# Cross-attention over 32 batches on one core: the issue order of five engines for batches 2 to 30 taken from one table

## The chip, the cores and the metric

The kernel runs on one core of one Trainium2 chip. The core has TensorE (PE; its weight loads are listed as PEld), VectorE (DVE), ScalarE (ACT), GpSimd (POOL) and SyncE (SP); here nearly all transfers are started from SP's queue. The metric is device time in microseconds, and less is better. Each engine works through its own instructions in the order in which the program lists them, and waits at an instruction until what it needs from the others is there.

## The reference

`x` has 32 batches of 512 rows by 640 columns, the context 32 by 77 rows by 1024 columns. All 77 context rows are text, so of the reference's four attentions three run over no rows at all, and their contribution is nothing. What is left:

```python
residual = hidden_states
q = _heads(hidden_states @ to_q_w)            # 20 heads of 32
h_txt = _sdpa(q, _heads(ehs_txt @ to_k_w), _heads(ehs_txt @ to_v_w))
...
out = _merge(h_txt) + SCALE_OBJ * _merge(h_obj) + SCALE_OTH * _merge(h_oth) + SCALE_IP * _merge(h_ip)
out = out @ to_out_w + to_out_b
out = (out + residual) / RESCALE
```

with `_sdpa` the softmax of q.k / sqrt(32) over the 77 keys, times v.

## The kernel before, in words

**Numbers.** Each operand of a product is kept as a high part in the reduced format `fp32r` and a low part, the rest; a product is three matmuls, high by high, high by low and low by high (`PAIRS`). An operation "high" copies (a cast), an operation "low" subtracts.

**Stages.** First the context's keys and values are made for all batches and put to DRAM (`k_dram`, `v_dram`). Then the 32 batches run, each in five chunks of 128 columns, four heads each: chunk n = 5 b + j, one call of `slot(n)` each (L688 to L825). At last `end()` drains what still runs behind.

**One chunk.** A chunk's work lies over several slots, so a slot holds work of several chunks:

- *Queries* of the next chunk, `queries(n + 1)` (L437): five steps of three matmuls of 512 columns into `pq`. `split_q` (L451) then makes `qt`: a cast of the whole on ACT (L454), two half copies on POOL (L458), two half subtractions on DVE (L460).
- *Scores* of this chunk, `scores(n, t)` (L464) for four row tiles t: three short matmuls into a bank `sc` (three banks), then the maximum on DVE (L486). `exps` (L491): four exponentials on ACT into `pn`, each with its sum.
- *Probabilities* of chunk n - 1: reciprocals on DVE (`sums`, L506), `normalize` on POOL (L511), `transpose_p` (L515): a transposition in blocks on DVE into the one buffer `z` (L518), four stores to DRAM (`pd`, L525).
- *Rows* of chunk n - 3 come back with `load_p` (L531, two transfers into `raw`). Of chunk n - 4: `cast_p` on ACT (L542, L543), `last_p` on POOL (L556), `rest_p` on DVE (L549) make `pp`.
- *Values* of chunk n - 4 (L564): six passes of 512 columns into `pa`. `sum_a` (L578): a copy `aw` of the lower half on ACT (L581) and two additions on DVE (L583). One slot later `high_a` (L585) on ACT and `low_a` (L593, L595) on DVE make `at`, which also empties `pa` (one buffer).
- *Output* of an earlier batch: 40 steps of three matmuls of 320 columns (`project`, L611) into two banks `po`, eight steps a slot in two pieces; batch b - 1 in chunks 3 and 4, batch b - 2 in chunks 0 to 2. A closed bank is added to the residual on DVE (L642) and stored.
- *x of the next batch*: loaded in four quarters into the one buffer `xs` (L253), turned in four parts on DVE (`transpose_x`, L257), split on ACT (L264) and POOL (L265).
- *Keys and values* of a group of chunks are reloaded in many small transfers (L419, L432); POOL copies two blocks of the keys (L423, L424).

**What sets the order.** `tc.manual_schedule` makes the order of the calls the order on each engine. In `slot` PE has: a score triple, two query steps, a triple, three query steps, a triple, then a piece of output, the values, a triple and a second piece of output. In chunks 1 and 4 the first piece stands one place earlier. Each of these groups is issued in one go. On DVE, `rest_p` stands before `low_a`, except in chunk 4. `load_p` stands in the middle of the slot, and the casts of its rows at the start of the next.

Of the kernel before, what the change touches and what calls it, by code (L numbers as in the profile page):

```python
# [51 lines left out]
def kernel(  # L52
# [358 lines left out]
    def load_keys(b, g, heads=range(HPC)):  # L411
        j0, nj = GROUPS[g]
        src = k_dram[g][:, :, :, b * NKEY : (b + 1) * NKEY].bitcast(F32)
        kb = kbs[g].bitcast(F32)
        for i in heads:
            own, half = slice(i * HD, (i + 1) * HD), slice(i % 2 * NKEY, (i % 2 + 1) * NKEY)
            other = slice(*((i + 2) % HPC * HD + k for k in (0, HD)))
            for part, rows in enumerate((own, other)):
                nc.sync.dma_start(kb[rows, 1 + i // 2, :, half], src[own, part])  # L419

    def copy_keys(g):
        kb = kbs[g]
        nc.gpsimd.tensor_copy(kb[:64, 0], kb[:64, 1].bitcast(F32))  # L423
        nc.gpsimd.tensor_copy(kb[64:, 3], kb[64:, 2].bitcast(F32))  # L424
# [39 lines left out]
    def scores(n, t):  # L464
# [6 lines left out]
        for m, (cols, keys_) in enumerate(  # L471
            (
                (slice(0, KCOLS), kb[:, 0::3, jg]),
                (slice(0, half), kb[:, 1, jg]),
                (slice(half, KCOLS), kb[:, 2, jg]),
            )
        ):
            nc.tensor.matmul(  # L478
                sc[:, cols],
                qt[:, m, t * P : (t + 1) * P],  # L480
                keys_,
                start=(m == 0),
                stop=(m == 2),
            )
# [30 lines left out]
    def transpose_p(n):  # L515

# [5 lines left out]
        pd = dram.tile([(NBLK + 2) * Q, S], F32, tag="pd", name="pd", bufs=6)  # L522
        rows = pd[: NBLK * Q].rearrange("(b i) q -> i b q", i=Q)
        for a in range(4):
            nc.sync.dma_start(  # L525
                rows[:, :, a * P : (a + 1) * P],
                z[a * Q : (a + 1) * Q].rearrange("p b t j -> p b (t j)"),
            )
        pds[n] = pd

    def load_p(n):  # L531
        pd = pds.pop(n)
        raw = late[0].tile([P, 3, S], F32, tag="raw", name="raw", bufs=2)
        nc.sync.dma_start(raw[:, 0:2, :], pd.rearrange("(k p) q -> p k q", k=2)[:P])
        nc.sync.dma_start(raw[:64, 2, :], pd[P : P + 64, :])
        raws[n] = raw

    def cast_p(n):

        raw = raws[n]  # L540
        pp = late[0].tile([P, 5, S], FPR, tag="pp", name="pp", bufs=1)
        nc.scalar.copy(pp[:64, 4, :], raw[:64, 2, :])  # L542
        nc.scalar.copy(pp[:, 0:2, :], raw[:, 0:2, :])  # L543
# [20 lines left out]
    def values(n):  # L564
        b, j = divmod(n, NC_)
        g = GROUP_OF[j]
        pp, vb = pps.pop(n), vbs[g][:, j - GROUPS[g][0]]
        pas[n] = late[1].tile([P, 2, S], F32, tag="pa", name="pa", bufs=1)
        for p, t, c in PASSES:
            nc.tensor.matmul(  # L570
                pas[n][:, p, :],
                vb[:, p, t, :],
                pp[:, c, :],
                start=(c == p),
                stop=(c == p + 2),
            )

    def sum_a(n):  # L578
        pa = pas[n]
        aw = late[0].tile([64, 2, S], F32, tag="aw", name="aw", bufs=1)  # L580
        nc.scalar.copy(aw, pa[64:])  # L581
        for p in range(2):
            nc.vector.tensor_tensor(pa[64 * p : 64 * p + 64, 0], pa[:64, p], aw[:, p], ALU.add)  # L583
# [9 lines left out]
    def low_a(n):  # L593
        at = ats[n]
        nc.vector.tensor_tensor(  # L595
            at[:, 1, :], pas.pop(n)[:, 0], at[:, 0, :].bitcast(F32), ALU.subtract
# [38 lines left out]

    def finish():

        while closed:
# [3 lines left out]
            nc.vector.tensor_tensor(  # L642
                xr[:, cols], pos.pop((b, t, h))[:, :HALF], xr[:, cols], ALU.add
            )
# [181 lines left out]

    def end():
# [105 lines left out]
    for n in range(LATE, N):  # L933
# [42 lines left out]
```

## Time and profile before

| what | value |
|---|---|
| runs | 1919.91, 1916.11, 1912.5 us |
| median | 1916.11 us |
| span of the profiled execution | 1928.2 us (its own time outside the span is not recorded) |
| mean granted TensorE clock | 0.995 |
| HBM traffic over the span | 222 GB/s |

Span and busy times are of one execution under the profiler, from its first to its last instruction. A row of groups reads: line, engine, operation, output<-inputs, shapes, count, then busy us and mean ns of one, then the idle time of the engine before them and what ended it. The chain of waits that ended last gives these shares of the span:

```profile
PE 38%; DMA 22%; ACT 14%; DVE 9%; SPq 7%; POOL 5%; issue 5%; ACTq 0%; DVEq 0%; POOLq 0%
```

No single engine or line holds it: it changes hands between all of them.

### The profile page before, as it was taken

What the parts mean: (1) busy time and instruction counts of PE and PEld (TensorE: products, weight loads), DVE (VectorE), ACT (ScalarE), POOL (GpSimd) and SP (SyncE); (2) the same over time, 40 slices, a digit from 0 to 9 for tenths busy, and PEclk for the clock granted to TensorE, in tenths of its full rate; (3) what the DMA queues carried; (4) which work ended last, traced back from release to release, by engine and by line L of the source; (5) the groups of instructions that cost most, each with busy time, mean ns of one, the idle gap of its engine ahead of it and who ended that gap; (6) DMA issues with size and microseconds to landing.
All of it is one profiled execution on the core that took longest, in us unless ns stands there. A gap on an engine that the chain in (4) does not pass through costs nothing.

```text
span 1928.2 us, 37543 instructions
## 1 busy us (share of the span) xinstructions
PE 1882.9 (98%) x10332; PEld 1663.1 (86%) x10332; DVE 1619.6 (84%) x2494; ACT 1527.4 (79%) x6210; POOL 1423.9 (74%) x1116
## 2 busy tenths in 40 slices
PE   9999997999999999999999999999999999999997
PEld 7888896898888888888888888988888888888887
DVE  4444447899999999999999999999999899999885
ACT  3232248998889898898898889998999889989883
POOL 1100067888888888888888888888888888888874
PEclk9999998999999999999999999999999999999999
DMA  9978868989999899888998998988889989988875
GB/s 185 205 194 248 198 180 218 229 232 234 233 225 235 231 232 225 229 234 231 233 231 228 228 238 236 237 231 232 237 232 227 228 223 232 227 231 229 225 202 166
DMA packets 565022, 431.36 MB, mean 224 GB/s; under 512 B 191120, under 2 KB 473168, under 8 KB 564816
## 3 DMA queue, kind: packets, MB, share of 16 engines
q1 hardware_dynamic: 559760, 413.62, 84.9%
q0 software_dynamic: 4416, 14.34, 2.2%
q8 instruction: 85, 1.39, 0.3%
q14 instruction: 121, 0.99, 0.2%
q10 hardware_dynamic: 640, 1.02, 0.2%
HBM read 247.17 MB, written 181.64 MB: 222 GB/s over the span
## 4 chain that ended last, share of the span: by engine, by line
PE 38%; DMA 22%; ACT 14%; DVE 9%; SPq 7%; POOL 5%; issue 5%; ACTq 0%; DVEq 0%; POOLq 0%
PE po L613 10%; PE pq L443 9%; DMA raw<-pd 8%; DMA xs<-in_x_dram 7%; ACT pn L496 6%; PE pv L191 5%; PE pk L191 5%; PE pa L570 4%; PE sc L478 4%; DVE pp L549 3%; DMA kb<-k_dram 2%; ACT pp L543 2%; SPq L432 2%; ACT pp L542 1%; ACT xt L264 1%
## 5 line engine op out<-in xcount | busy, mean ns | idle before, releaser
L496 ACT ACTIVATE pn<-sc,nm 128x77 f32<-128x77 f32 x2560 | 793.8, 332 | 46.6 <-DVE nm L486 40.6
L613 PE MATMUL po<-wo_s,at 128*128 128x320 f32 x3840 | 635.1, 314 | 12.1 <-DVE at L595 9.0
L443 PE MATMUL pq<-xt,wq_s 128*128 128x512 f32 x2400 | 623.7, 401 | 0.0
L613 PEld LDWEIGHTS po<-wo_s,at 128*128 128x128 f32 x3840 | 568.3, 189 | 20.4 <-DVE at L595 17.4
L496 ACT ACTIVATION_READ_ACCUMULATOR pn<-sc,nm 128x1 f32 x2560 | 544.6, 213 | 0.0
L511 POOL TENSOR_TENSOR pn<-pn,rs 128x1232 f32<-128x1232 f32 x160 | 507.7, 3173 | 33.3 <-DVE rs L506 24.2
L443 PEld LDWEIGHTS pq<-xt,wq_s 128*128 128x128 f32 x2400 | 431.3, 190 | 76.1
L478 PEld LDWEIGHTS sc<-kb,qt 128*128 128x128 f32 x1920 | 327.8, 189 | 57.2 <-POOL qt L458 8.7
L478 PE MATMUL sc<-kb,qt 128*128 128x154 f32 (+1 forms) x1920 | 318.1, 274 | 11.0 <-POOL qt L458 4.5
L486 DVE TENSOR_REDUCE nm<-sc 128x4 f32<-128x308 f32 x640 | 287.7, 450 | 37.7 <-PE sc L478 33.2
L549 DVE TENSOR_TENSOR pp<-raw,pp 128x1024 fp32r<-128x1024 f32 x160 | 253.1, 1582 | 40.7 <-ACT pp L543 38.7
L556 POOL TENSOR_TENSOR pp<-raw,pp 64x512 fp32r<-64x512 f32 x160 | 209.3, 1308 | 100.2 <-ACT pp L542 90.5
L570 PE MATMUL pa<-pp,vb 128*128 128x512 f32 x960 | 263.7, 404 | 15.3 <-DVE at L595 10.1
L518 DVE STREAM_TRANSPOSE z<-pn 128x1280 f32<-128x1280 f32 x160 | 241.8, 1511 | 9.3 <-DMA pd<-z 2.7
L460 DVE TENSOR_TENSOR qt<-pq,qt 64x512 fp32r<-64x512 f32 x320 | 219.1, 685 | 29.0 <-ACT qt L454 22.7
L583 DVE TENSOR_TENSOR pa<-pa,aw 64x512 f32<-64x512 f32 x320 | 222.6, 696 | 24.3 <-ACT aw L581 14.0
L265 POOL TENSOR_TENSOR xt<-xs,xt 128x512 fp32r<-128x512 f32 x160 | 202.6, 1291 | 37.1 <-ACT xt L264 32.5
L570 PEld LDWEIGHTS pa<-pp,vb 128*128 128x128 f32 x960 | 169.7, 188 | 63.4 <-DVE pp L549 15.4
L606 POOL TENSOR_TENSOR xr<-xr,bias 128x640 f32<-128x640 f32 x128 | 202.7, 1585 | 17.3 <-DMA xr<-in_x_dram 5.4
L458 POOL CAST qt<-qt 64x512 fp32r<-64x512 f32 x320 | 194.8, 609 | 23.7 <-ACT qt L454 4.2
L581 ACT COPY aw<-pa 64x1024 f32<-64x1024 f32 x160 | 161.9, 1012 | 48.2 <-PE pa L570 44.1
L542 ACT CAST pp<-raw 64x512 fp32r<-64x512 f32 x160 | 99.5, 622 | 99.7 <-DMA raw<-pd 95.6
(46 smaller groups left out, 1640.9 us busy)
## 6 DMA issues: line engine op xcount, KB each, us to landing
pd<-z SPq DMA_DIRECT2D x640, 160.0 KB, 3.5
raw<-pd SPq DMA_DIRECT2D x160, 512.0 KB, 4.3
xs<-in_x_dram SPq DMA_DIRECT2D x128, 320.0 KB, 7.4
xr<-in_x_dram SPq DMA_DIRECT2D x128, 320.0 KB, 3.7
out_dram<-xr SPq DMA_DIRECT2D x127, 320.0 KB, 3.7
raw<-pd SPq DMA_DIRECT2D x160, 128.0 KB, 4.3
v_dram<-vs SPq DMA_DIRECT2D x80, 192.0 KB, 4.0
k_dram<-ks POOLq DMA_DIRECT2D x20, 512.0 KB, 4.2
```

What stands on the lines that cost most here:

```text
L443: nc.tensor.matmul(pqs[n], wq_s[:, k, a, j * P : (j + 1) * P], xts[b, k][:, c, :], start=(k == 0 and m == 0), stop=(k == NC_ - 1 and m == 2),)
L460: nc.vector.tensor_tensor(qt[r, 1 + w, :], pq[r], qt[r, 0, :].bitcast(F32), ALU.subtract)
L478: nc.tensor.matmul(sc[:, cols], qt[:, m, t * P : (t + 1) * P], keys_, start=(m == 0), stop=(m == 2),)
L486: nc.vector.tensor_reduce(nm, sc[:, :KCOLS].rearrange("p (h k) -> p h k", k=NKEY), AX.X, ALU.max, negate=True)
L496: nc.scalar.activation(pnb[n % 2][:, at, :NKEY], sc[:, i * NKEY : (i + 1) * NKEY], AF.Exp, bias=nm[:, i : i + 1], accum_out=sms[n][:, at : ...
L511: nc.gpsimd.tensor_tensor(pf, pf, rs.unsqueeze(2).to_broadcast([P, NQ * HPC, NKEY]), ALU.mult)
L518: nc.vector.transpose(z.rearrange("p b t j -> p t b j"), pn.rearrange("p (t h) k -> p t (h k)", t=NQ).rearrange("p t (b i) -> p t b i", i=Q),)
L549: nc.vector.tensor_tensor(pp[:, 2:4, :], raw[:, 0:2, :], pp[:, 0:2, :].bitcast(F32), ALU.subtract)
L556: nc.gpsimd.tensor_tensor(pp[64:, 4, :], raw[:64, 2, :], pp[:64, 4, :].bitcast(F32), ALU.subtract)
L570: nc.tensor.matmul(pas[n][:, p, :], vb[:, p, t, :], pp[:, c, :], start=(c == p), stop=(c == p + 2),)
L583: nc.vector.tensor_tensor(pa[64 * p : 64 * p + 64, 0], pa[:64, p], aw[:, p], ALU.add)
L613: nc.tensor.matmul(pos[b, t, h][:, :HALF], ats[b * NC_ + j][:, a, t * P : (t + 1) * P], wos[0][:, j, c, h * HALF : (h + 1) * HALF], start= ...
```

## The change

`slot` stays for chunks 0 to 9 and for the last batch. For batches 2 to 30 a table `PLAN` of 344 steps is walked once a batch, and `issue` carries out each. A step is the chunk j (0 to 4), a letter, and arguments. To make single steps possible, several helpers are cut in two or more (`split_x` into `high_x` and `low_x`, `scores` into `score_tile` and `score_max`, `load_keys` by head and part, `transpose_p` into `block_transpose` and `store_p`, `values` into `value_pass`, `sum_a` into `lower_half` and `add_halves`, `finish` into `add_output` and `store_output`); what each does is the same as before.

Letters: `q` a query step of the next chunk, `s` a score triple, `v` a value pass, `p` an output step by its number in `STEPS`; `m` maximum, `e` exponentials, `r` reciprocals, `N` normalize, `z` block transposition, `w` a store of it; `d` load of rows (0: 512 KB, 1: 128 KB), `c` cast of rows, `l` `last_p`, `R` `rest_p`; `A` and `a` `sum_a` in its parts, `h` and `L` high and low of `at` of chunk n - 5; `Q`, `k`, `g` the parts of `split_q`; `f` and `o` addition and store of the output, `b` bias; `T`, `X`, `x` turn and split of x; `K` copy of keys; `ur`, `ux`, `uk`, `uv` loads of residual, x, keys and values.

```diff
+    PLAN = (
+        "0p16 0s0 0q0 0s1 0m0 0q1 0h 1uv13 0r 0m1 0c1 0N 0q2 0L 0d0 1uv16 0p17 0e0 0f10 0d1 0q3 0R "
+        "0uk101 0s2 0c0 0uk100 0q4 0m2 0ux3 0v1 0l 0Q 0uk130 0v0 0p18 0e1 0g1 0p19 0p20 0k0 0g0 0s3 "
+        "0e2 0v2 0f11 0k1 0v4 0m3 0v3 0o1 0p21 0b2 0z 0uk110 0v5 1q0 0uk111 0A 1s0 1s1 0w1 0e3 0a1 "
+        "1q1 0w3 0T0 0p22 0w2 1q2 1c0 1d0 1r 0a0 1c1 0w0 1q3 1l 1m0 1uv12 1T1 0p23 1h 1uv17 1q4 1e0 "
+        "1m1 1N 1uv15 1L 1p24 0ur3 1s2 1R 1d1 1Q 1p25 1uv14 1e1 1s3 1v0 1m2 1v1 1v3 1m3 1p26 1e2 "
+        "1uv10 1g0 1k1 1v5 1p27 0uk120 1f20 1k0 1v2 1uv11 1g1 1e3 1p28 2d0 1v4 1z 0uk131 1p30 1b3 2s0 "
+        "1A 2s1 2q0 2r 1w2 2c0 1a0 2q1 1ur0 2c1 2l 0uk121 1a1 2s2 2d1 1p31 2m0 2h 1w1 2q2 2m1 2e0 2N "
+        "1w0 2m2 2q3 2L 2uv06 2q4 2R 2e1 1p29 2v0 2f21 2s3 2Q 2v1 1T2 3uk030 2e2 2p32 2k0 1w3 2v2 2g0 "
+        "2p35 2o2 2k1 2v3 2T3 2v4 1K11 3uk021 2v5 2p33 2g1 3uk020 1K10 2A 2p36 2b0 2uv03 2m3 2p37 "
+        "2uv07 2X0 2p38 2a0 3uk011 2X1 3q0 3d0 2z 2x0 3c1 3d1 3s0 3q1 2e3 2x1 2p34 2w0 2a1 3s1 2w2 "
+        "3m0 2p39 3c0 3uk031 2f30 3q2 3m1 3h 2uv01 3l 3r 3q3 3e0 3L 2w1 3uk000 3q4 3N 2w3 3X2 3s2 "
+        "2uv00 3p0 3X3 3m2 3s3 3f31 3Q 3v0 3R 3v1 3o3 3e1 3v3 3uk001 3p4 2uv02 3p1 3g0 4d0 3p5 3e2 "
+        "3k1 2uv05 3p6 3g1 3k0 3v2 2uv04 3p2 3z 3X4 4K01 4d1 3v5 3p7 3x2 3v4 4s0 3m3 3A 3w3 3p3 3x3 "
+        "3w0 4q0 3w1 3e3 3a1 4q1 3w2 3x4 3a0 4s1 3ur1 4q2 4m0 3uk010 4h 4r 4m1 4ur2 4c0 4s2 4L 4q3 "
+        "4ux0 4c1 4l 4ux1 4p8 4e0 4ux2 4p9 4f00 4q4 4N 4m2 4f01 4p10 4Q 4R 4o0 4v1 4e1 4v0 4v2 4p11 "
+        "4g0 4v3 4p12 4e2 4g1 4p13 4k0 4s3 4z 4v5 4K00 4v4 4p14 4A 4k1 4p15 4m3 4w2 4b1 4a0 4e3 4w0 "
+        "4w3 4a1 4w1 "
+    ).split()
+    ADDED = {4: 1, 0: 2, 1: 2, 2: 2, 3: 2}
+    OPEN = [(B - 3, 1, 0)]
+
+    scs, nms, rss = {}, {}, {}
+
+    def issue(b, token):
+
+        j, op, arg = int(token[0]), token[1], [int(c) for c in token[2:] if c.isdigit()]
+        n, kind = b * NC_ + j, token[2:3]
+        old, out_b = n - LAG, b - PIECES[j][0]
+        half = (slice(0, 64), slice(64, P))
+        if op == "q":
+            queries(n + 1, arg[0], arg[0] + 1)
+        elif op == "s":
+            scs[n, arg[0]] = score_tile(n, arg[0])
+        elif op == "m":
+            nms[n, arg[0]] = score_max(scs[n, arg[0]])
+        elif op == "e":
+            exps(n, arg[0], scs.pop((n, arg[0])), nms.pop((n, arg[0])))
+        elif op == "r":
+            rss[n - 1] = sums(n - 1)
+        elif op == "N":
+            normalize(n - 1, rss.pop(n - 1))
+        elif op == "z":
+            block_transpose(n - 1)
+        elif op == "w":
+            store_p(n - 1, arg[0])
+        elif op == "d":
+            load_rows(n - LAG + 1, arg[0])
+        elif op == "c":
+            cast_rows(old, arg[0])
+        elif op == "l":
+            last_p(old)
+        elif op == "R":
+            rest_p(old)
+        elif op == "v":
+            value_pass(old, arg[0])
+        elif op == "A":
+            lower_half(old)
+        elif op == "a":
+            add_halves(old, arg[0])
+        elif op == "h":
+            high_a(old - 1)
+        elif op == "L":
+            low_a(old - 1)
+        elif op == "Q":
+            nc.scalar.copy(qts[(n + 1) % 2][:, 0, :], pqs[n + 1])
+        elif op == "k":
+            qt, w = qts[(n + 1) % 2], arg[0]
+            nc.gpsimd.tensor_copy(qt[half[1 - w], 1 + w, :], qt[half[w], 0, :].bitcast(F32))
+        elif op == "g":
+            qt, w = qts[(n + 1) % 2], arg[0]
+            nc.vector.tensor_tensor(
+                qt[half[w], 1 + w, :], pqs[n + 1][half[w]], qt[half[w], 0, :].bitcast(F32), ALU.subtract
+            )
+        elif op == "p":
+            t, h, c = STEPS[arg[0] if len(arg) == 1 else 10 * arg[0] + arg[1]]
+            if c == 0:
+                output_bank(out_b, t, h)
+            project(out_b, t, h, c)
+        elif op == "f":
+            add_output(b - ADDED[j], *arg)
+        elif op == "o":
+            store_output(b - ADDED[j], arg[0])
+        elif op == "b":
+            add_bias(b - BIAS[j][0], arg[0])
+        elif op == "T":
+            transpose_x(b + 1, arg[0])
+        elif op == "X":
+            high_x(b + 1, arg[0])
+        elif op == "x":
+            low_x(b + 1, arg[0])
+        elif op == "K":
+            copy_half_keys(*arg)
+        elif kind == "r":
+            load_residual(b - RESIDUAL[j][0], arg[0])
+        elif kind == "x":
+            ahead = 1 if arg[0] == 3 else 2
+            if b + ahead < B:
+                load_x(b + ahead, arg)
+        elif kind == "k":
+            load_head_keys(b + 1 if j == 3 else b, *arg)
+        elif kind == "v":
+            load_values(b - 1 if j == 1 else b, arg[0], SEGMENTS[arg[1] : arg[1] + 1])
+
```

The loop:

```diff
-    for n in range(LATE, N):
+    for n in range(LATE, 2 * NC_):
+        slot(n)
+    for b in range(2, B - 1):
+        while closed:
+            closed.pop()
+        for token in PLAN:
+            issue(b, token)
+    closed.extend(OPEN)
+    for n in range(N - NC_, N):
         slot(n)
     end()
```

On PE the query steps, output steps, value passes and triples now stand singly or in short runs between each other. The second piece of output is not kept in order of its steps everywhere: chunk 3 has 0, 4, 1, 5, 6, 2, 7, 3, and chunk 2 has 32, 35, 33, 36, 37, 38, 34, 39. Value passes and additions change places with their neighbours in some chunks. `rest_p` stands behind `low_a` in all chunks. On SP the four stores of `z`, the loads of rows, and the loads of keys and values are spread between each other, one transfer a step.

More of the change, by code (lines that the diff above doesn't have):

```diff
@@ L562, with value_pass, values, lower_half @@
     PASSES = [(p, t, c + p * (t == 0)) for t, c in ((0, 0), (1, 4), (0, 2)) for p in range(2)]
[L564 removed]
+    def value_pass(n, i):
         b, j = divmod(n, NC_)
         g = GROUP_OF[j]
[L567 to L576, printed above, removed]
[L578 to L583 removed]
+        pp, vb = pps[n], vbs[g][:, j - GROUPS[g][0]]
+        if n not in pas:
+            pas[n] = late[1].tile([P, 2, S], F32, tag="pa", name="pa", bufs=1)
+        p, t, c = PASSES[i]
+        nc.tensor.matmul(
+            pas[n][:, p, :],
+            vb[:, p, t, :],
+            pp[:, c, :],
+            start=(c == p),
+            stop=(c == p + 2),
+        )
+    def values(n):
+        for i in range(len(PASSES)):
+            value_pass(n, i)
+    def lower_half(n):
+        aws[n] = late[0].tile([64, 2, S], F32, tag="aw", name="aw", bufs=1)
+        nc.scalar.copy(aws[n], pas[n][64:])
+    def add_halves(n, p):
+        pa, aw = pas[n], aws[n]
+        nc.vector.tensor_tensor(pa[64 * p : 64 * p + 64, 0], pa[:64, p], aw[:, p], ALU.add)
+    def sum_a(n):
+        lower_half(n)
+        add_halves(n, 0)
+        add_halves(n, 1)
     def high_a(n):
```

119 lines of the change are left out of this document (77 added, 42 removed).

## The prediction

> **What bounds the kernel now.** I read the page's first part, then the windows by stage, then TensorE (PE) in order of time, then the waits of the steady stretch, 400 to 1800 us, which is clear of the opening (keys and values for all batches) and of the tail.
>
> ```profile
> PE 1882.9 (98%) x10332; PEld 1663.1 (86%) x10332; DVE 1619.6 (84%) x2494; ACT 1527.4 (79%) x6210; POOL 1423.9 (74%) x1116
> ```
>
> PE is the engine to look at. Two windows over the steady stretch, the first for products into `po` alone (PE, PEld and DVE busy), the second for everything (PE, PEld, DVE, ACT, POOL busy; granted clock, DMA share, GB/s):
>
> ```profile
> 400.00:1800.00 1400.00, 549.90 (x3321) 489.94 (x3321) 101.47 (x222) 1.00 0.90 231
> ...
> 400.00:1800.00 1400.00, 1382.88 (x7884) 1233.37 (x7884) 1294.04 (x1993) 1253.68 (x5258) 1196.39 (x913) 1.00 0.90 231
> ```
>
> A batch has 40 steps of 3 output products, so 3321/120 = 27.7 batches lie in 1400 us: **50.6 us a batch**. Per batch DVE is busy 46.7, ACT 45.3, POOL 43.2 us, the DMA engines 0.90 of the time; the clock was 1.00, so no clock gain is to be had. Nothing beside PE binds by its sum, but DVE has under 4 us to spare.
>
> How much of the 50.6 is products? A busy PE overstates it, because matmul ends are modelled, so I go by starts (columns: start us, us, engine, line, shapes, count):
>
> ```profile
> 1006.44 1.56 PE L570 MATMUL pa<-pp,vb 128*128 128x512 f32 x6
> 1007.84 0.48 PE L478 MATMUL sc<-kb,qt 128*128 128x308 f32 x3
> 1008.15 1.96 PE L613 MATMUL po<-wo_s,at 128*128 128x320 f32 x12
> 1009.95 0.49 PE L478 MATMUL sc<-kb,qt 128*128 128x308 f32 x3
> 1010.28 1.59 PE L443 MATMUL pq<-xt,wq_s 128*128 128x512 f32 x6
> 1011.71 0.50 PE L478 MATMUL sc<-kb,qt 128*128 128x308 f32 x3
> 1012.04 2.26 PE L443 MATMUL pq<-xt,wq_s 128*128 128x512 f32 x9
> 1014.14 0.49 PE L478 MATMUL sc<-kb,qt 128*128 128x308 f32 x3
> ```
>
> From start to next start: 6 value passes 1.40, 12 output products 1.80, 6 query products 1.43, 9 of them 2.10, a score triple about 0.325. A chunk is 15 query, 24 output, 6 value products and 4 triples: 1.43 + 2.10 + 2 x 1.80 + 1.40 + 4 x 0.325 = 9.83 us; five are 49.2 us. So **PE stands still about 1.4 us a batch**. Where, is told by one stop in order of time and by the waits of the steady stretch (waited for: us, times, longest):
>
> ```profile
> 1055.45 1.81 PE L613 MATMUL po<-wo_s,at 128*128 128x320 f32 x11
> 1057.62 0.41 PE L613 MATMUL po<-wo_s,at 128*128 128x320 f32 x1 [0.36 <-DVE at L595]
> ```
>
> ```profile
> ACT pp L542 <- DMA raw<-pd: 88.9, 78, 3.0
> POOL kb L424 <- DMA kb<-k_dram: 72.3, 28, 4.1
> ...
> PEld po L613 <- DVE at L595: 14.4, 24, 1.4
> PEld pa L570 <- DVE pp L549: 14.0, 28, 0.6
> ...
> PEld pa L570 <- DVE at L595: 10.4, 21, 1.8
> ...
> PEld pa L570 <- POOL pp L556: 2.1, 4, 0.8
> ```
>
> Three places: output products of chunk 3 that need the low part of `at` just made (`low_a`, L595); value passes of chunks 1 and 2 that need `pa` emptied by the same line; value passes of chunk 4 that come before `rest_p` (L549) is through. ACT and POOL wait too, for rows and keys from DRAM, and so run late into these.
>
> **The change, part by part.** No arithmetic is added, no transfer, no product: all counts stay. What moves is the order on each engine and on SP's queue, for batches 2 to 30 (29 of 32). So the most that PE can gain is 29 x 1.4 = 41 us, and each edit is priced by what PE has between a producer and its user.
>
> *Output steps and `low_a`, chunk 3.* Step 3 (chunk 3's input) was fourth; in the table `3L` is followed by one query step, two triples, seven other output steps, six passes and another triple before `3p3`: 0.7 + 0.65 + 7 x 0.45 + 1.4 + 0.33 = 6.2 us of PE. `3L` costs 0.68. This stop goes.
>
> *Passes behind `low_a`.* Between `1L` and `1v0`: two output steps, two triples, 1.55 us; between `2L` and `2v0`: two query steps and an output step, 1.85 us. The rest of DVE that stands ahead of `L` counts too, below.
>
> *Passes behind `rest_p`, chunk 4.* The passes are split: `4v1 4v0 4v2 4v3` and three output steps and a triple stand between `4R` and `4v5`: 0.93 + 1.35 + 0.33 = 2.6 us against 1.6 for L549. Goes.
>
> *Rows and keys.* Counting the PE steps between them in the table, loads `d` stand five to thirteen us ahead of their casts `c`, against 4.4 to 9.8 us for the slowest kind of load, x (rows below); the 88.9 and 72.3 us of waits on ACT and POOL (3.2 and 2.6 us a batch) turn into spare time. That cover is what lets the steps above be early; alone it moves PE by nothing.
>
> *The new waits.* `2s0`, the first triple of chunk 2, reads what `1g1` writes, and everything PE has left is queued behind it. I add up DVE from there back. Its groups in the steady stretch, with mean ns, then how closely two follow:
>
> ```profile
> L486 DVE TENSOR_REDUCE nm<-sc 128x4 f32<-128x308 f32 x554 | 248.8, 449 | 28.0 <-PE sc L478 24.0
> ...
> L549 DVE TENSOR_TENSOR pp<-raw,pp 128x1024 fp32r<-128x1024 f32 x138 | 220.1, 1595 | 36.1 <-ACT pp L543 34.3 <-DMA pd<-z 1.6
> L518 DVE STREAM_TRANSPOSE z<-pn 128x1280 f32<-128x1280 f32 x138 | 208.6, 1511 | 6.5 <-DMA pd<-z 1.2 <-POOL xr L606 0.9
> L583 DVE TENSOR_TENSOR pa<-pa,aw 64x512 f32<-64x512 f32 x276 | 192.0, 696 | 9.0
> L460 DVE TENSOR_TENSOR qt<-pq,qt 64x512 fp32r<-64x512 f32 x278 | 190.3, 684 | 20.2 <-ACT qt L454 14.7
> ...
> L581 ACT COPY aw<-pa 64x1024 f32<-64x1024 f32 x139 | 140.6, 1012 | 24.7 <-PE pa L570 21.0 <-PE sc L478 1.1
> L642 DVE TENSOR_TENSOR xr<-po,xr 128x320 f32<-128x320 f32 x222 | 101.5, 467 | 0.0
> L595 DVE TENSOR_TENSOR at<-pa,at 128x512 fp32r<-128x512 f32 x139 | 94.5, 680 | 5.8 <-ACT at L590 5.8
> L257 DVE STREAM_TRANSPOSE xs<-xs 128x640 f32<-128x640 f32 x110 | 91.0, 827 | 0.0
> ```
>
> ```profile
> L506 DVE RECIPROCAL rs<-sm 128x16 f32<-128x16 f32 x160 | 37.0, 231 | 0.4
> ```
>
> ```profile
> 1031.15 1.43 DVE L583 TENSOR_TENSOR pa<-pa,aw 64x512 f32<-64x512 f32 x2
> 1032.49 0.83 DVE L257 STREAM_TRANSPOSE xs<-xs 128x640 f32<-128x640 f32 x1
> ```
>
> Two of L583 take 1.34 from start to start, so one follows 0.03 to 0.08 us before the last has ended. From `0T0` to `1g1` stand 2 x 0.83, 0.23 (reciprocal, the last row), 0.70, 4 x 0.45, 0.68, 1.60, 2 x 0.68 and 0.47, which is 8.5, with overlap 7.6 to 8.2. Before them the copy `0A` (1.0, after `0v5`) and `0a1` (0.7). From the end of `0v5` to `2s0` PE has one full chunk, 9.83. That is 9.3 to 9.9 plus a few tenths of handing over: the slack is about **0.2 us**, and this holds only if `0T0` does not wait.
>
> It may. `0T0` turns part of the next batch's x, whose fourth quarter `0ux3` is issued on SP behind four stores of `z` and six more transfers, all after `4z`:
>
> ```profile
> 1010.64 2.90 SPq L525 DMA_DIRECT2D pd<-z  x4
> 1013.65 0.43 SPq L534 DMA_DIRECT2D raw<-pd  x1
> 1014.12 0.58 SPq L535 DMA_DIRECT2D raw<-pd  x1
> ...
> 1021.03 2.27 SPq L525 DMA_DIRECT2D pd<-z  x4
> ```
>
> ```profile
> DMA to landing us min/median/max: 4.4/7.5/9.8
> ...
> DMA to landing us min/median/max: 5.9/5.9/5.9
> ...
> DMA to landing us min/median/max: 5.0/5.0/5.0
> ```
>
> (The first landing line is of all x loads of the steady stretch, the other two of a fourth quarter alone, issued at 1024 and at 1075 us.) Four stores take 2.3 to 2.9 us to issue, six more about 0.5 each: 5.6. With the 5.0 to 5.9 of a fourth quarter x is there 10.6 to 11.5 us after `4z`. DVE between `4z` and `0T0`: five L486, three L583, two L642, L595, L549, two L460, one L518 and a reciprocal, 10.6 us, with overlap 9.6 to 10.3, and about 0.4 of waiting for `0Q` and `0A`: 10.0 to 10.7. So `0T0` waits 0 to 1.5 us, I take 0.7; less the slack of 0.2 that is a stop of 0.5 a batch. With a landing at 7.5, the median of all x loads, the wait is 2.7.
>
> [...]
>
> *Other tight spots.* Between `4L` (0.68) and `4p8`, which reads it, PE has one query step, 0.7; between POOL's `4k1` and `0s0` two output steps, 0.9, but `4k1` is last behind `4l`, `4N`, `4k0` and `4K00`. From below they cost nothing, if those covers hold; from above, what such waits cost before on the PEld rows: 14.4 and 10.4 us over 27.7 batches, 0.5 and 0.4 a batch. I take 0.25 for both, nearer to nothing, since each still has a step as cover.
>
> **Sum.** 1.4 - 0.5 - 0.25 = 0.65 us a batch; x 29 = 19 us. The profiled execution spans 1928.2 us; the median of the runs is 1916.11, or 0.9937 of it. (1928.2 - 19) x 0.9937 = 1897 us.
>
> **Rivals.** *All stops gone* (x lands by 10 us, DVE keeps its overlap): 1.4 x 29 = 41, 1928.2 - 41 = 1887, x 0.9937 = 1875 us. For it: the least landing, 4.4; against it: DVE without a gap over half a batch.
>
> *One set of stops for another:* `0T0` waits about 1.3 and PE stops 1.1 + 0.25 a batch, as much as before: 1915 us. For it: DVE's ten groups at their upper end with a landing of 6.
>
> *Slower, by the fourth quarter of x.* If `0ux3` lands 7.5 us after issue, because loads of rows now lie ahead of it on the same transfer engines, DVE stands 2.7 us in front of `0T0`; the reciprocal, hence POOL's normalization, and `1m0`, hence the exponentials, are late with it, and PE stops 2.5 + 0.25 a batch. That is 1.35 more than before: 39 us, (1928.2 + 39) x 0.9937 = 1955 us. It loses from a landing of 6.3 us on. Against it: the fourth quarter landed in 5.9 where the other three took longer.
>
> *Shorter spacing:* mixing long and short products could let weight loads hide better, until DVE's 46.7 us a batch binds: (50.6 - 46.7) x 29 = 113, so 1804 us. Against it: in the rows 512-column products start 0.233 to 0.24 apart, both in runs of their own kind and before a triple. [...]
>
> **How the numbers follow.** Forecast 0.40 (own range 1886 to 1907); all stops gone 0.20; one set for another 0.21; slower by x 0.17; shorter spacing 0.02. About 0.5%, 9.6 us, is what a measurement of this kernel can tell from no change. Faster by more: 0.38 of the forecast's 0.40, with 0.20 and 0.02, is 0.60. Within: 0.22. Slower: 0.18. The range is from 1873, a little below all stops gone, to 1935, half of the slower case's loss; it leaves out the spacing, and most of the slower case, some 0.16 in all.
>
> **What would show it.** Right: DVE's wait for `low_a` gone from PE's waits; ACT's wait for `raw` and POOL's for `kb` near nothing; a batch at about 50 us by the count of `po`; a wait of DVE's `xs` transposition on its transfer of 0.3 to 1.5 us a batch; `sc` waiting on L460's `qt`. Wrong: start-to-start times of products that differ from before; a wait of DVE on `xs` over 2 us; PE waiting on POOL's `qt` or on `sc` buffers instead.

## The result, and the profile after

| what | before | after |
|---|---|---|
| median of 4 runs each | 1914.79 us (1912.5 to 1919.91) | 1948.82 us (1947.86 to 1950.86) |
| ratio, with its 95% interval | 1 | 1.0164 (1.0135 to 1.0193) |
| span of the profiled execution | 1928.2 us | 1946.7 us |

The kernel became slower by 1.6%. On a second chip the loss was smaller, 1.0094 (1.0072 to 1.0116). The page's first part of the kernel after:

```profile
PE 1891.3 (97%) x10332; PEld 1668.3 (86%) x10332; DVE 1688.5 (87%) x2494; ACT 1522.4 (78%) x6210; POOL 1371.7 (70%) x1116
```

The counts are those of before. Yet DVE is busy 69 us longer with the same 2494 instructions, and POOL 52 us less with the same 1116. The steady stretch, 400 to 1800 us, first for `po` alone, then for everything, in the columns of the prediction:

```profile
400.00:1800.00 1400.00, 618.01 (x3288) 531.27 (x3288) 103.97 (x218) 1.00 0.86 228
...
400.00:1800.00 1400.00, 1373.25 (x7792) 1221.94 (x7791) 1343.10 (x1964) 1232.36 (x5187) 1135.58 (x904) 1.00 0.86 228
```

3288/120 = 27.4 batches, so **51.1 us a batch** against 50.6; over 29 batches that is 14.5 of the 18.5 us of span. DVE is busy 1343.10/27.4 = 49.0 us of the 51.1. Which instruction became longer, the groups of that stretch tell (after, then the counterpart of before, whose L549 is in the prediction):

```profile
L535 POOL TENSOR_TENSOR pn<-pn,rs 128x1232 f32<-128x1232 f32 x137 | 313.3, 2287 | 59.8 <-DVE rs L530 51.1
L589 DVE TENSOR_TENSOR pp<-raw,pp 128x1024 fp32r<-128x1024 f32 x137 | 302.0, 2205 | 0.0
L952 POOL CAST qt<-qt 64x512 fp32r<-64x512 f32 x274 | 240.3, 877 | 37.5 <-ACT qt L949 25.4
```

```profile
L511 POOL TENSOR_TENSOR pn<-pn,rs 128x1232 f32<-128x1232 f32 x139 | 446.1, 3210 | 20.0 <-DVE rs L506 12.1
L458 POOL CAST qt<-qt 64x512 fp32r<-64x512 f32 x276 | 168.1, 609 | 17.0
```

The same `rest_p` on the same shape takes 2205 ns instead of 1595; the same `normalize` takes 2287 instead of 3210. What one has lost the other has won. The spread in each kernel, from the view of one tile (minimum, median, maximum in ns; before, then after), says that neither mean is the operation's own price:

```profile
L549 DVE TENSOR_TENSOR pp<-raw,pp x138: 1198/1518/2362, 408.3 to 1795.1; 128x1024 fp32r<-128x1024 f32 x138
```

```profile
L589 DVE TENSOR_TENSOR pp<-raw,pp x137: 1197/2189/2971, 399.6 to 1793.5; 128x1024 fp32r<-128x1024 f32 x137
```

In order of time the two kernels show who waits. Before, POOL and then DVE:

```profile
1023.13 3.45 POOL L511 TENSOR_TENSOR pn<-pn,rs 128x1232 f32<-128x1232 f32 x1 [0.19 <-DVE rs L506]
...
1023.24 1.20 DVE L549 TENSOR_TENSOR pp<-raw,pp 128x1024 fp32r<-128x1024 f32 x1
```

After, in the same order:

```profile
1024.09 2.27 POOL L535 TENSOR_TENSOR pn<-pn,rs 128x1232 f32<-128x1232 f32 x1
1026.43 1.48 POOL L952 CAST qt<-qt 64x512 fp32r<-64x512 f32 x1
...
1024.89 2.55 DVE L589 TENSOR_TENSOR pp<-raw,pp 128x1024 fp32r<-128x1024 f32 x1
1027.37 1.40 DVE L955 TENSOR_TENSOR qt<-pq,qt 64x512 fp32r<-64x512 f32 x2
```

Before, `rest_p` is through in 1.20 us, and `normalize`, recorded from about the same moment, ends 3.45 us after its start. After, `rest_p` comes 0.80 us behind `normalize` and ends at 1027.44, that is 1.08 us after `normalize` has ended at 1026.36; and the cast behind `normalize` takes 1.48 instead of 0.61, since it waits for the rest of `rest_p`. The theory that I tested, called **exclusion** below: `rest_p` and an instruction on POOL (in these rows `normalize` and the cast) do not run at the same time. Whichever is second waits for the whole of the other, and the wait is recorded as part of its own duration (2205 ns of L589 on the mean), not as idle time (0.0 us in its row).

Its price on DVE: `rest_p` alone takes 1.21 (below). Five a batch at 2.205 are 5.0 us of waiting, at 1.595 before 1.9 us. So 3.1 us a batch of waiting came onto DVE, the engine that had under 4 to spare. POOL, which had 7, was rid of 4.6 at `normalize` (5 x 0.92) and got 2.7 back at the ten casts behind it (877 instead of 609 ns).

Where PE pays, from the waits of the steady stretch of after:

```profile
PEld po L664 <- DVE xr L689: 26.6, 52, 1.1
PEld pa L611 <- POOL pp L596: 19.3, 27, 0.8
...
PEld pa L611 <- DVE pp L589: 7.5, 26, 0.3
...
DVE xs L257 <- DMA xs<-in_x_dram: 1.1, 1, 1.1
...
POOL kb L437 <- DMA kb<-k_dram: 0.3, 1, 0.3
...
ACT pp L578 <- DMA raw<-pd: 0.2, 1, 0.2
```

PEld and PE record the same stop, so I add only PEld's rows: 26.6 + 19.3 + 7.5 = 53.4, with the short rows left out here 55.1, over 27.4 batches is 2.0 us a batch, and 49.2 + 2.0 is about the 51.1 found. (Before, 14.4 + 14.0 + 10.4 + 2.1 = 40.9 over 27.7, 1.5 a batch.) Two of the stops in order of time, and behind them the `rest_p` and the `last_p` ahead of the first:

```profile
1037.29 0.97 PE L611 MATMUL pa<-pp,vb 128*128 128x512 f32 x3 [0.53 <-POOL pp L596]
...
1052.06 2.23 PE L460 MATMUL pq<-xt,wq_s 128*128 128x512 f32 x9
1054.13 0.60 PE L664 MATMUL po<-wo_s,at 128*128 128x320 f32 x3
1054.57 0.39 PE L611 MATMUL pa<-pp,vb 128*128 128x512 f32 x1
...
1056.59 0.70 PE L664 MATMUL po<-wo_s,at 128*128 128x320 f32 x3 [0.36 <-DVE xr L689]
...
1033.92 2.19 DVE L589 TENSOR_TENSOR pp<-raw,pp 128x1024 fp32r<-128x1024 f32 x1
...
1035.57 1.67 POOL L596 TENSOR_TENSOR pp<-raw,pp 64x512 fp32r<-64x512 f32 x1 [0.55 <-ACT pp L578]
```

The first is `0v2`, behind `last_p` of chunk 0. That `last_p` waited 0.55 us for its rows' cast and then took 1.67 us instead of 1.29, because `rest_p`, itself held by `normalize`, was at work until 1036.11. The second is `2p35`, which needs a `po` bank that the addition `2f21` empties, and `2f21` stands right behind `2R` on DVE, which lasts until 1056.14. The rows between show that the products keep their spacing: nine query products in 2.07 us, three output products in 0.44, against the 2.10 and 0.45 (a quarter of the 1.80 for twelve) of the prediction.

### The profile page after: what moved, and what is told of

Read it like the earlier page. It is cut to its first block, busy times and chain, and to the rows that moved or that the text cites. A ratio compares the mean times of both kernels' runs of the same rounds, so it can differ in the third digit from the quotient of the medians.

```text
span 1946.7 us, 37371 instructions
## 1 busy us (share of the span) xinstructions
PE 1891.3 (97%) x10332; PEld 1668.3 (86%) x10332; DVE 1688.5 (87%) x2494; ACT 1522.4 (78%) x6210; POOL 1371.7 (70%) x1116
## 4 chain that ended last, share of the span: by engine, by line
PE 42%; DVE 30%; DMA 10%; issue 8%; SPq 5%; ACT 3%; POOL 2%; DVEq 0%; ACTq 0%; POOLq 0%
PE po L664 13%; PE pq L460 10%; DVE pp L589 6%; PE pk L191 6%; PE pv L191 5%; DVE nm L506 5%; DVE qt L955 5%; DVE z L541 4%; PE pa L611 4%; PE sc L495 4%; DMA pd<-z 4%; DVE pa L629 3%; DVE xr L689 3%; SPq L550 3%; DVE at L646 2%
## 5 line engine op out<-in xcount | busy, mean ns | idle before, releaser
L520 ACT ACTIVATE pn<-sc,nm 128x77 f32<-128x77 f32 x2560 | 796.2, 339 | 89.3 <-DVE nm L506 86.8
L664 PE MATMUL po<-wo_s,at 128*128 128x320 f32 x3840 | 714.1, 313 | 14.6 <-DVE xr L689 11.1
L664 PEld LDWEIGHTS po<-wo_s,at 128*128 128x128 f32 x3840 | 617.9, 189 | 80.1 <-DVE xr L689 28.5
L460 PE MATMUL pq<-xt,wq_s 128*128 128x512 f32 x2400 | 653.7, 399 | 0.0
L520 ACT ACTIVATION_READ_ACCUMULATOR pn<-sc,nm 128x1 f32 x2560 | 562.0, 220 | 0.0
L460 PEld LDWEIGHTS pq<-xt,wq_s 128*128 128x128 f32 x2400 | 424.9, 190 | 59.6
L535 POOL TENSOR_TENSOR pn<-pn,rs 128x1232 f32<-128x1232 f32 x160 | 374.4, 2340 | 75.2 <-DVE rs L530 65.5
L611 PE MATMUL pa<-pp,vb 128*128 128x512 f32 x960 | 325.2, 410 | 22.0 <-POOL pp L596 17.8
L589 DVE TENSOR_TENSOR pp<-raw,pp 128x1024 fp32r<-128x1024 f32 x160 | 341.0, 2132 | 4.1 <-ACT pp L580 3.9
L596 POOL TENSOR_TENSOR pp<-raw,pp 64x512 fp32r<-64x512 f32 x160 | 217.4, 1359 | 144.6 <-ACT pp L578 100.9
L952 POOL CAST qt<-qt 64x512 fp32r<-64x512 f32 x290 | 253.5, 874 | 40.2 <-ACT qt L949 27.4
L271 POOL TENSOR_TENSOR xt<-xs,xt 128x512 fp32r<-128x512 f32 x160 | 202.6, 1290 | 34.6 <-ACT xt L267 32.0
L955 DVE TENSOR_TENSOR qt<-pq,qt 64x512 fp32r<-64x512 f32 x290 | 197.6, 681 | 4.9
L580 ACT CAST pp<-raw 128x1024 fp32r<-128x1024 f32 x160 | 168.2, 1051 | 0.0
```

What stands on the lines that cost most here:

```text
L460: nc.tensor.matmul(pqs[n], wq_s[:, k, a, j * P : (j + 1) * P], xts[b, k][:, c, :], start=(k == 0 and m == 0), stop=(k == NC_ - 1 and m == 2),)
L520: nc.scalar.activation(pnb[n % 2][:, at, :NKEY], sc[:, i * NKEY : (i + 1) * NKEY], AF.Exp, bias=nm[:, i : i + 1], accum_out=sms[n][:, at : ...
L535: nc.gpsimd.tensor_tensor(pf, pf, rs.unsqueeze(2).to_broadcast([P, NQ * HPC, NKEY]), ALU.mult)
L589: nc.vector.tensor_tensor(pp[:, 2:4, :], raw[:, 0:2, :], pp[:, 0:2, :].bitcast(F32), ALU.subtract)
L611: nc.tensor.matmul(pas[n][:, p, :], vb[:, p, t, :], pp[:, c, :], start=(c == p), stop=(c == p + 2),)
L664: nc.tensor.matmul(pos[b, t, h][:, :HALF], ats[b * NC_ + j][:, a, t * P : (t + 1) * P], wos[0][:, j, c, h * HALF : (h + 1) * HALF], start= ...
```

## The experiments

A diff of bare steps shows the order on the engine named ahead of it; the other engines keep theirs. "Batch" is 1400 us over the number of batches by the count of `po`; "PEld" is the sum of all its waits per batch. The last two columns are means in the steady stretch, waits included; 2 x stands for two halves. Each ratio is to the kernel before on the same chip; the other columns are of one profiled execution of each run, on its own chip, and for before the one of the tables above.

| run | ratio (95%) | batch, us | PEld, us | `rest_p`, ns | `normalize`, ns |
|---|---|---|---|---|---|
| before | 1 | 50.6 | 1.5 | 1595 | 3210 |
| after | 1.0164 (1.0135 to 1.0193) | 51.1 | 2.0 | 2205 | 2287 |
| after_again | 1.0094 (1.0072 to 1.0116) | 51.1 | 2.1 | 2218 | 2277 |
| late_rest | 0.9964 (0.9949 to 0.9979) | 50.5 | 1.2 | 1838 | 2279 |
| rest_first | 1.0009 (0.9992 to 1.0026) | 50.6 | 1.2 | 1558 | 2277 |
| no_norm | 0.9793 (0.9767 to 0.9819) | 49.2 | 0.0 | 1211 | left out |
| before_swapped | 1.0492 (1.0463 to 1.0521) | 54.1 | 5.5 | 2564 | 2497 |
| before_first | 1.0506 (1.0471 to 1.054) | 53.9 | 3.5 | 1506 | 2275 |
| combo_a | 0.9884 (0.9858 to 0.991) | 50.0 | 0.6 | 1639 | 2277 |
| combo_b | 0.9822 (0.9791 to 0.9852) | 49.4 | 0.1 | 1443 | 2279 |
| split_norm | 0.9837 (0.9818 to 0.9855) | 49.5 | 0.1 | 1487 | 2 x 1652 |
| before_split | 0.9997 (0.9978 to 1.0017) | 50.7 | 1.8 | 1580 | 2 x 1685 |
| combo_split | 0.9872 (0.9838 to 0.9905) | 50.0 | 0.6 | 1314 | 2 x 1334 |

**The two operations alone** (the attention is left out; `rest_p`, `normalize` and short operations are issued in several orders).

```diff
...
+    for k in range(10):
+        norm(k)
+        small(2)
+        rest()
+        small(8)
+    for k in range(10):
+        norm(k)
+        rest()
+        small(8)
...
```

> The two operations by themselves, ten times each in six settings: rest_p alone; normalize alone; normalize begun, two small DVE operations later rest_p; normalize and rest_p released at the same time; rest_p first, normalize released by a reciprocal behind it; normalize begun, two small operations later the two subtractions of split_q, which read PSUM. The rest of the kernel is left out. Exclusion: alone 1.2 and 2.28 us; in the third setting rest_p ends 1.1 us after normalize's end and normalize takes 2.28; in the fourth one of the two waits for the other in full; in the last the subtractions take 0.69 us as ever. Hand-over (or a shared bandwidth in place of exclusion): in the third setting both take longer, or neither does.

In order of time, the first two rows are of the first loop, the next two of the second; then `rest_p` ahead of the reciprocal; last two subtractions L93 that read PSUM and SBUF, beside `normalize`:

```profile
98.22 2.26 POOL L86 TENSOR_TENSOR pn<-pn,rs 128x1232 f32<-128x1232 f32 x1 [1.84 <-DVE rs L84]
98.86 2.70 DVE L81 TENSOR_TENSOR pp<-raw,pp 128x1024 fp32r<-128x1024 f32 x1
...
174.21 1.16 DVE L81 TENSOR_TENSOR pp<-raw,pp 128x1024 fp32r<-128x1024 f32 x1
174.43 3.05 POOL L86 TENSOR_TENSOR pn<-pn,rs 128x1232 f32<-128x1232 f32 x1 [5.36 <-DVE rs L84]
...
226.13 1.21 DVE L81 TENSOR_TENSOR pp<-raw,pp 128x1024 fp32r<-128x1024 f32 x1
...
304.76 2.26 POOL L86 TENSOR_TENSOR pn<-pn,rs 128x1232 f32<-128x1232 f32 x1 [4.26 <-DVE rs L84]
305.38 1.38 DVE L93 TENSOR_TENSOR qt<-sc,qt 64x512 fp32r<-64x512 f32 x2
```

Alone they take 1.21 and 2.26. If `normalize` has begun, `rest_p` takes 2.70 and ends 1.08 us after `normalize`, as in the kernel; if `rest_p` is 0.22 us ahead, it takes 1.16 and `normalize` 3.05. No other engine worked beside the two (ACT has no instruction, PE one matmul, at 1.45 us), so no other load explains it. Subtractions with one operand in PSUM (`rest_p` has both in SBUF) take 0.69 each beside `normalize`, against the 0.68 of L460 in the kernel before, and `normalize` keeps its 2.26. So of these two operations the second waits for the first, 1.49 us on DVE and 0.79 on POOL; where the recorded starts lie only 0.1 us apart, they do not tell who was first (last section).

**Without `normalize`** (left out in batches 2 to 30, so that the probabilities there stay undivided).

```diff
         elif op == "N":
-            normalize(n - 1, rss.pop(n - 1))
+            rss.pop(n - 1)
```

> The changed kernel without normalize in batches 2 to 30 (the probabilities stay undivided there), order untouched. Exclusion: rest_p's mean 1.2 to 1.4 us, a batch 49.3 to 49.8 us, time 1890 to 1908 us. Hand-over: it takes 11 us a batch off POOL alone, so the stops that last_p ends go (0.8 us a batch) but those behind DVE's additions stay: a batch about 50.4, time 1920 to 1930 us.

```profile
L589 DVE TENSOR_TENSOR pp<-raw,pp 128x1024 fp32r<-128x1024 f32 x143 | 173.1, 1211 | 0.7 <-issue 0.7
```

`rest_p` is back at its own price, PE has no stop of note left (0.5 us in the whole stretch), and the batch takes the 49.2 us that were added up as the floor. This run also takes 11 us a batch of work off POOL, so by itself it doesn't single out the exclusion; the halves below do.

**`rest_p` later in chunks 2 and 4** (DVE).

```diff
-2L 2R 2f21 1T2 2g0
+2L 1T2 2f21 2R 2g0
-4f01 4R 4g0 4g1 4z
+4f01 4g0 4g1 4R 4z
```

> In the changed kernel rest_p (L589) takes 2205 ns on the mean where it took 1595, and normalize on POOL 2287 where it took 3210. Theory 'exclusion': the two cannot work at the same time; the one that starts second waits, and now that is rest_p, on DVE, which has no time to spare. Theory 'hand-over': rest_p's length is a side show; finely mixed products make PE wait for single hand-overs (accumulators closed on DVE, value passes behind POOL's last_p), and would do so with a short rest_p too. This run changes only DVE's order in two of five chunks: in chunk 2 rest_p goes behind transpose_x and the addition of the output, in chunk 4 behind the two subtractions of split_q, so that normalize is over or nearly over. Exclusion: rest_p falls to 1.2 to 1.6 us in these two chunks, its mean to 1.8 to 1.9 us; a batch from 51.2 to 50.2 to 50.7 us; time 1920 to 1935 us. Hand-over: 1945 to 1955 us.

The waits on L596 and most of those on L689 are gone. Of the 26.4 us behind `rest_p`, 18 lie at `4v5`, a pass behind the late `4R`, and 8 at `1v5`:

```profile
PEld pa L611 <- DVE pp L589: 26.4, 56, 0.8
...
PEld po L664 <- DVE xr L689: 7.6, 28, 0.3
```

**Besides, `rest_p` ahead of the reciprocal in chunks 1 and 3** (DVE).

```diff
-0T0 1r 0a0 1m0 1T1 1m1 1L 1R 1m2
+0T0 0a0 1m0 1T1 1R 1r 1L 1m1 1m2
-2a1 3m0
+2a1 3R 3m0
-3f31 3R 3g0
+3f31 3g0
```

> As late_rest, and in chunk 1 the reciprocal (which normalize waits for) stands behind rest_p, in chunk 3 rest_p stands five places earlier, before normalize can begin. Exclusion: rest_p's mean falls to 1.3 to 1.6 us, normalize's rises or keeps; DVE busy per batch from 49 to 46 us; a batch 49.6 to 50.2 us; time 1900 to 1920 us. Hand-over: 1940 to 1955 us.

`rest_p` became as short as expected, 1558 ns, but the time, 1935.24 us, missed the 1900 to 1920 expected. In chunk 3 it now meets another POOL instruction, the low part of x (the last row is of PE's waits):

```profile
1003.98 1.90 DVE L589 TENSOR_TENSOR pp<-raw,pp 128x1024 fp32r<-128x1024 f32 x1
...
1002.26 2.53 POOL L271 TENSOR_TENSOR xt<-xs,xt 128x512 fp32r<-128x512 f32 x2
1004.87 2.15 POOL L596 TENSOR_TENSOR pp<-raw,pp 64x512 fp32r<-64x512 f32 x1
...
PEld sc L495 <- ACT pn L520: 15.8, 27, 0.6
```

L271 lasts until 1004.79 and holds `3R`, which in turn holds `last_p` (2.15 instead of 1.29). The maximum `3m0` behind `3R` is late, the exponentials with it, and PE waits for a score bank, 15.8 us in all on ACT's L520; the stop at `4v5` also stays, most of 14.8 us behind L589. The mean of `rest_p` alone was no measure of the gain: what is queued behind it decides.

**Before, with `rest_p` and `low_a` exchanged in chunks 0 to 3, as the table has them.**

```diff
-        if taken is not None:
-            rest_p(taken)
         if j != NC_ - 1 and n - 1 in takes:
             low_a(takes[n - 1])
+        if taken is not None:
+            rest_p(taken)
```

> The kernel before with two neighbours on DVE exchanged in chunks 0 to 3: low_a first, then rest_p, as the changed kernel has it. Exclusion: rest_p starts some 0.6 us later, when normalize has begun, and waits for it: rest_p's mean from 1.6 to 1.9 to 2.2 us, normalize's from 3.2 to 2.3 to 2.7 us, time 1920 to 1945 us. Hand-over: the products that waited for low_a get it earlier, time 1900 to 1915 us.

```profile
L549 DVE TENSOR_TENSOR pp<-raw,pp 128x1024 fp32r<-128x1024 f32 x130 | 333.3, 2564 | 9.7 <-ACT pp L543 9.7
```

```profile
PEld pa L570 <- DVE pp L549: 117.7, 98, 2.3
```

The sign and the place are as the exclusion has them: `normalize` falls from 3210 to 2497, `rest_p` rises to 2564. The loss of 4.9% was far beyond the expected size. The second row, of the waits, says where: `slot` issues the six passes in one go, and they wait for `rest_p` up to 2.3 us at a time. In the table, output and query products stand between them.

**Before, with `rest_p` ahead of the reciprocal** (a first part of the diff, which only lets `rest_p` read its rows without taking them off a list, is left out).

```diff
+        if taken is not None:
+            rest_p(taken)
         rs = sums(n - 1) if n else None
...
-        if taken is not None:
-            rest_p(taken)
```

> The kernel before with rest_p on DVE moved up to stand ahead of the reciprocal that normalize waits for, so that normalize can only begin when rest_p is over. Exclusion: normalize takes 2.28 us instead of 3.2, rest_p 1.2 us, or up to 2.2 where it must wait for last_p: mean 1.2 to 1.6; if the reciprocal is not held up, the batch gets 0.2 to 0.8 us shorter, ratio to before 0.984 to 0.998. Hand-over: the reciprocal, hence normalize, gets later for nothing, ratio 1.000 to 1.010.

```profile
POOL pn L511 <- DVE rs L506: 209.7, 128, 2.5
PEld po L613 <- DVE at L595: 87.9, 52, 2.7
...
DVE pp L549 <- ACT pp L543: 73.4, 51, 3.0
```

`normalize` is at 2275, so the exclusion between these two is gone, and still the kernel is slower by 5%, where 0.2 to 1.6% faster was expected: on DVE `rest_p` waits for ACT's cast of its rows (up to 3.0 us), and the reciprocal and `low_a`, which stand behind it in DVE's order, come late with it: POOL waits for the one up to 2.5 us, PE for the other up to 2.7. An order that avoids one wait is worth nothing if the moved instruction is not ready at its new place.

**`late_rest`, and cover for its last stops** (DVE, then PE).

```diff
-3f31 3R 3g0 3g1
+3f31 3g0 3R 3g1
-4s3 4v5 4v4 4p14 4p15
+4s3 4p14 4v5 4v4 4p15
```

> late_rest (ratio 0.9964, batch 50.5 us with PE stops of 0.3 us at the fifth pass of chunk 1, 0.2 at the first output step behind an addition, 0.76 at the fifth pass of chunk 4, all behind rest_p) with two further moves: in chunk 4 an output step goes ahead of the two passes that wait for rest_p, in chunk 3 half of split_q goes ahead of rest_p. Exclusion: the 0.76 shrinks to 0 to 0.3, the rest stays: a batch 49.9 to 50.2 us, ratio 0.982 to 0.992. Hand-over: the stop moves to the next pass, ratio 0.994 to 1.000.

**The same, and chunk 1 of `rest_first`** (the first of its pairs above).

> combo_a and in chunk 1 the reciprocal behind rest_p, as in rest_first (there rest_p of chunk 1 took 1.18 us and no stop stood in chunk 1). Exclusion: the remaining 0.5 us of stops in chunk 1 and at the handover to chunk 2 go, a batch 49.4 to 49.7 us, ratio 0.974 to 0.985. Hand-over: as combo_a.

Both came out as expected, 0.9884 and 0.9822. Of all waits of PE and PEld in combo_b, only these come to more than 0.4 us in all over the whole stretch:

```profile
PEld pa L611 <- DVE pp L589: 3.2, 10, 0.7
...
PE pa L611 <- DVE pp L589: 0.7, 2, 0.4
```

**`normalize` in two halves, the table untouched.**

```diff
-        nc.gpsimd.tensor_tensor(
-            pf, pf, rs.unsqueeze(2).to_broadcast([P, NQ * HPC, NKEY]), ALU.mult
-        )
+        half = NQ * HPC // 2
+        for k in range(0, 2 * half, half):
+            part = pf[:, k : k + half]
+            nc.gpsimd.tensor_tensor(
+                part, part, rs[:, k : k + half].unsqueeze(2).to_broadcast([P, half, NKEY]), ALU.mult
+            )
```

> The changed kernel, its table untouched, with normalize as two POOL instructions of half the columns each. Exclusion held for a whole instruction: rest_p, issued 0.8 to 1.2 us after the first half began, waits only for that half's end and goes between the two: mean 1.3 to 1.7 us instead of 2.2, the second half takes 1.2 us longer; a batch 49.7 to 50.4 us, ratio to before 0.982 to 0.998. Bandwidth shared over the overlap, or hand-over on PE as the cause: rest_p stays near 2.2 us, ratio 1.013 to 1.020, or more for the added instruction.

```profile
1014.13 1.21 DVE L592 TENSOR_TENSOR pp<-raw,pp 128x1024 fp32r<-128x1024 f32 x1
...
1012.97 3.46 POOL L538 TENSOR_TENSOR pn<-pn,rs 128x616 f32<-128x616 f32 x2 [0.62 <-DVE rs L530]
```

No step of the table moved, no arithmetic changed, POOL got an instruction more in each chunk; the ratio went from 1.0094 to 0.9837 on one chip (1950.77 and 1900.76 us). `rest_p`, begun 1.16 us into `normalize`, now waits for the half in progress at most, and here slips in between: 1.21 us, and the second half carries the wait. So the wait is for the one instruction in progress, and the length of `normalize` was what the table lost its time to. **The kernel after, run on the same chip:**

> The changed kernel once more, beside the next: ratio to before 1.013 to 1.020 as measured, since a ratio should carry from chip to chip though the time does not (before took 1915 us on one chip and 1934 us on another).

It took 1950.77 us against 1932.51 of before there: 1.0094, below the 1.013 to 1.020 expected, so the ratio did not carry from chip to chip either.

**The halves in the kernel before, and in combo_b.**

> The kernel before, its order untouched, with normalize in two halves. In two chunks of five rest_p began just behind normalize and went first (1.2 us), in the others it had waited for last_p, and normalize waited for it. Exclusion: rest_p and the batch change little, since rest_p waits little for normalize here; normalize's two halves take one more start: ratio 0.993 to 1.005. If halves were good in themselves: 0.98 to 0.99, as in the changed kernel. It also tells what the table's order is worth once the wait is out of both: split_norm's ratio of 0.984 against this one.

> combo_b (ratio 0.982, batch 49.5 us, where TensorE's products alone take 49.3) with normalize in two halves. Exclusion and PE as the bound: at most the last 0.2 us a batch to gain, ratio 0.979 to 0.985. If the two cures add up: 0.970 or less.

In the old order the halves gain nothing (0.9997), as expected: there `normalize` did the waiting already (3210 ns against 2277 to 2287 in the new order). So the table is worth about 1.6% once the wait is out of it. In combo_b they gain nothing: 0.9872 is above the 0.979 to 0.985 expected, though its interval and that of combo_b's 0.9822, from another chip, overlap. The cures do not add up. In the trace small stops come back, mostly at `4v5` and `0v2` (11.3 us of PEld behind L592, 9.0 of them at `4v5`, and 5.9 behind `last_p`), though `rest_p` fell to 1314 ns. In chunk 4 it overlaps a cast of keys on POOL, as it does in combo_b (1.36 and 1.45 us instead of 0.57); why PE loses was not followed further.

## Why the prediction was wrong

The forecast was 1897 us, faster, with a range up to 1935; the median was 1948.82. Step by step:

- **The floor** of 49.2 us a batch was right: no_norm reached it, without a stop.
- **The old stops.** That behind `low_a`, for output steps and for passes, went as said: no row with L646 is left among PE's waits. The waits for rows and keys went from 88.9 and 72.3 us to 0.2 and 0.3. The stop of chunk 4's passes behind `rest_p`, 14.0 us, went too, although `rest_p` took longer. (Between `2L` and `2v0` the table has one query step and one output step, 1.15 us, not the 1.85 that were added up; nothing hung on it.)
- **The new waits: the step that failed.** In the sum of DVE's work, and in the cover for passes behind `rest_p`, L549 was put at 1.60, the mean in the trace of before, as if that were what the operation takes. It is 1.21 plus a wait for POOL, and after the change it was 2.2. The exchange of `rest_p` with `low_a`, told ahead of the prediction, got no price at all. Moved behind `low_a` and the additions, `rest_p` begins 0.8 us and more after `normalize`, not beside it, and so takes over the wait. That is 0.61 us more than the sum had, five times a batch, on an engine with under 4 us to spare. The place was wrong too: no stop of note lies at `2s0`, but 0.70 us a batch at `0v2`, a pass behind `last_p`, 0.97 at the output steps `2p35` and `1p30` behind additions, and 0.27 at `1v5`, a pass of chunk 1 behind `rest_p`.
- **The fourth quarter of x**, the wait that the prediction feared instead, was not there: DVE waited for x once, 1.1 us. `0ux3` was issued 5.3 to 6.4 us after the first of the four stores began, about as forecast, but in 25 of 27 batches it landed 3.7 to 4.7 us later, not 5.0 to 5.9 or more; the term of 0.5 us a batch was nothing. With it falls the mechanism of the slower rival, though its sign came true.
- **The other tight spots**, `4p8` and `0s0`, put at 0.25 us a batch, cost nothing: neither L646 nor L952 holds PE for more than 0.2 us in the stretch.
- **The sum** gave 50.6 - 0.65 = 49.95 us a batch, and 51.1 was measured: 1.15 x 29 = 33 us.
- **The way to the median** was the other miss. The factor 0.9937, from the span of before to its median, lowers 1909 us to 1897. After has 1946.7 as its span and 1948.82 as its median, 1.001. So of the 52 us of error some 14 are the factor and some 38 the span. The factor was no property of the kernel: in every run whose span and time are both on record the time is 1.7 to 2.2 us longer than the span, so the profiled execution of before, with 1928.2 us of span, took about 1930 (an estimate from these), more than any of the four timed on the first chip. Against it after is longer by 18.5 us or 1.0%, which is the 1.0094 of the second chip.

That all stops could go, 1875 us or 0.98 of before, was a case of the prediction; combo_b and split_norm come close to it (0.982 and 0.984). So the table was no worse an order; what it lost lay in the length of one POOL instruction that it let start first.

The trace of before had the sign in it: one instruction on one shape between 1198 and 2362 ns, and a `normalize` of 3.14 and 3.45 us beside it.

Open: before took 1914.79 us on the first chip and 1932 to 1937 (medians) on four others, while after took the same on two chips to 2 us. Which chip the profiled execution of before ran on is not recorded. So the traces account for a loss of 1.0%; why before was about 0.8% faster in the four runs on the first chip, which makes the loss 1.6% there, is not shown.

## What to carry to other kernels

Take an instruction's own price from its shortest records, and ask of every long one what it waited for: the wait inside `rest_p` (2205 ns instead of 1211) appears in no idle time. Here `rest_p`, with both operands in SBUF, and POOL's `normalize` waited for each other's end (2.70 us instead of 1.21, 3.05 instead of 2.26), and subtractions with one operand in PSUM did not wait (0.69). Where a trace shows such a pair, let the engine with time to spare be second, or cut the POOL instruction into pieces (1487 ns for `rest_p` instead of 2218, a ratio of 0.9837 instead of 1.0094). Look at what is queued behind a moved instruction before looking at the instruction itself.

## What the hardware showed besides

The recorded start did not decide who was first: before, `rest_p` began 0.11 us after `normalize`'s start in the record (1023.24 and 1023.13) and still went through at once. In split_norm, 0.24 us behind the first half (1005.58 and 1005.34), it took 2.07 us, so there it waited.

In before_first a stop of PE cost more than its length. One stop in order of time, and the clock in windows of 1 us around it (granted clock third from the end):

```profile
1058.07 0.50 PE L613 MATMUL po<-wo_s,at 128*128 128x320 f32 x2
1060.95 1.42 PE L613 MATMUL po<-wo_s,at 128*128 128x320 f32 x4 [2.38 <-DVE at L595]
1062.16 2.58 PE L570 MATMUL pa<-pp,vb 128*128 128x512 f32 x6
```

```profile
1060.00:1061.00 1.00, 0.05 (x1) 0.05 (x1) 1.00 (x4) 0.00 (x0) 0.51 (x1) 1.00 0.99 341
1061.00:1062.00 1.00, 1.00 (x4) 1.00 (x5) 1.00 (x3) 0.69 (x5) 1.00 (x1) 0.50 1.19 174
...
1064.00:1065.00 1.00, 1.00 (x7) 0.87 (x6) 0.56 (x1) 0.52 (x4) 0.92 (x2) 0.79 1.24 222
```

The six passes behind it take 2.42 us to the next start instead of 1.40. After 21 of the 25 such stops of the stretch the clock fell: here to 0.50 for about 3.4 us (from 1061 on three windows at 0.50 and one at 0.79), and around eight others a window of 10 us has the mean of the one from 1060 to 1070, 0.83. Over the stretch the mean is 0.97, which is 0.03 x 1400/26 = 1.6 us a batch (by 21 x 3.4 us at half speed, 1.4) beside the 3.5 of the stops. In the kernels before and after, where PE's longest recorded waits in the stretch are 1.6 and 0.8 us, it stayed at 1.00; in before_swapped, with 1.8, it fell once in the stretch, between 490 and 500 us (0.83). The length of a stop alone did not decide it: of 24 stops of 2.37 to 2.43 us in before_first 20 were followed by a fall and 4 were not, and the one of 1.59 us was.
